# Layer 2 of a four-layer image network: attention of one image issued beside the feed forward of the image ahead, in a fixed order

## The chip, the cores and the metric

The kernel runs on one core of a Trainium2 chip. The core has a matrix engine (TensorE, PE in the profile), a vector engine (VectorE, DVE), an activation engine (ScalarE, ACT), a general engine (GpSimd, POOL) and a queue for transfers (SyncE, SP). Each engine works through its own instructions in order and waits on semaphores for the others. The metric is the device time of one execution in microseconds (us); lower is better. All data are float32, and a product of two float32 matrices is issued as two passes of the matrix engine, so that the profile shows two MATMUL records for each matrix product that is written in the code.

## The reference, cut to what matters

Four layers run one after the other on an input of 4 images with 128 channels of 64 x 64 points: an attention layer, a layer of adder convolutions, the layer that is changed here (layer 2), and a state space layer. Layer 2 is this, for each image on its own:

```python
def _biasfree_ln(x, w):                       # over the 128 channels of a point
    mu = jnp.mean(x, axis=1, keepdims=True)
    var = jnp.mean((x - mu) ** 2, axis=1, keepdims=True)
    return x / jnp.sqrt(var + EPS) * w[None, :, None, None]

def _elgca_attn(x, dw_w, dw_b, qkvl_w, qkvl_b):
    x1, x2 = (x[:, :C2], x[:, C2:])           # C2 = 64 channels each
    x1 = _gelu(_conv(x1, dw_w, dw_b, groups=C2, pad=1))      # 3x3 depthwise
    x2 = _gelu(_conv(x2, qkvl_w, qkvl_b))                    # 64 -> 128 channels
    x2 = x2.reshape(B, HEADS, C4, H, W)                      # q, k, v, lfeat: 32 each
    ...
    qf = _avg_pool_3s2p1(q).reshape(B, C4, -1)
    kf = _max_pool_2s2(k).reshape(B, C4, -1)
    qk = jnp.einsum('bcn,bdn->bcd', qf, kf)                  # 32 x 32
    attn = jnp.swapaxes(jax.nn.softmax(qk, axis=1), 1, 2)
    out = jnp.einsum('bcd,bdn->bcn', attn, v).reshape(B, C4, H, W)
    return jnp.concatenate([x1, lfeat, out], axis=1)

def _elgca_mlp(x, fc1_w, fc1_b, pos_w, pos_b, fc2_w, fc2_b):
    h = _gelu(_conv(x, fc1_w, fc1_b))                        # 128 -> 512 channels
    h = h + _gelu(_conv(h, pos_w, pos_b, groups=h.shape[1], pad=1))
    return _conv(h, fc2_w, fc2_b)                            # 512 -> 128

h = _elgca_attn(_biasfree_ln(x, ln1_w), dw_w, dw_b, qkvl_w, qkvl_b)
out = h + x
return out + _elgca_mlp(_biasfree_ln(out, ln2_w), fc1_w, fc1_b, pos_w, pos_b, fc2_w, fc2_b)
```

## The kernel before, in words

Channels lie on the 128 partitions of the on-chip memory, and the 4096 points of an image along each partition. The four images stay there in tiles `x0` to `x3` (the argument `xp`, 16 KB on each partition) from the residual of layer 1 (`residual`, L578) to the preparation of layer 3 (`layer3_prepare`, L808). Layer 2 (L597 to L775) works in place on them. It loops over the images (L643), and for each image it writes down, in this order:

- The **first layer norm** (`layernorm`, L628) in 8 blocks of 512 points: a matrix product with a matrix of 1/128 gives the mean (`pm`, L633), DVE subtracts (L635), ACT squares (L636), a second product gives the variance (`pv`, L638), ACT takes Ln and Exp (`rstd`, L82 and L83), and DVE multiplies (L641) into the padded tile `hp`.
- The **attention**: 8 matrix products over the upper 64 channels and a Gelu on ACT give `x2` (L654, L657). DVE makes the depthwise convolution of the lower 64 channels in 9 taps over 64 partitions and 4096 points (L664, L666), then ACT makes its Gelu (L667). DVE pools q and k (L672 to L679); PE transposes the pooled maps (L684) and multiplies them (L690); a softmax over a 32 x 32 matrix follows (L694 to L703). DVE adds two parts of the result to the image (L705, L706), and PE and DVE make and add the third in 8 blocks (`po`, L709, and L713).
- The **second layer norm**, into the tile `m` (L716).
- The **feed forward**, in two halves of 32 rows and four chunks of 128 of the 512 channels: `up` is 5 matrix products with a Gelu each into the padded tile `ht` (L734, L737). The depthwise convolution of chunk 0 is made on PE, as 4 x 9 matrix products with diagonal matrices (L747) and a Gelu each (L754). That of chunks 1 to 3 is made on DVE in 9 taps of 128 partitions and 2048 points (L760, L762), with one Gelu on ACT (L765). DVE adds the centre (L766), and 4 matrix products sum the chunk into four banks of the matrix engine's memory (`pf2`, L770). At the end of a half DVE adds the four banks to the image (L775).

The order of instructions on each engine in layer 2 is set by a planner when the kernel is built: it goes by the order in the code as a priority and by estimated costs, and it may take instructions of the next image earlier. Layers 1 and 3 use `tc.keep_in_program_order`, here named `then`, which keeps the instructions given to it in the order of the code on each engine; instructions outside it can be placed freely. Buffers come from pools: `ps` has four banks for all products but the sums, `ps_f` four for the sums; the tiles `hp`, `x2`, `x1`, `cs`, `pf` and `m` exist once, and `ht` and `g` twice.

The activation engine holds one set of function tables at a time. `ln_and_exp` (L76) loads the set with Ln and Exp; a Gelu after it needs another load.

Of the kernel before, what the change touches and what calls it, by code (L numbers as in the profile page):

```python
# [1 line left out]

# [15 lines left out]
B = 4  # L18
# [36 lines left out]
def col(ap):  # L55

    return ap.rearrange("(p o) -> p o", o=1)
# [538 lines left out]

def layer2(tc, cm, xp, ln1, ln2, dw_w, dw_b, qkvl_w, qkvl_b, fc1_w, fc1_b, pos_w, pos_b, fc2_w, fc2_b):  # L597
    nc = tc.nc
    NCH = 4
    with ExitStack() as ctx:  # L600
# [3 lines left out]
        ps = ctx.enter_context(tc.tile_pool(name="l2p", bufs=4, space=PSUM))  # L604
# [8 lines left out]
        ln2_sb = load([1], col(ln2), "ln2")  # L613
        dww = load([TAPS], dw_w, "dww")
        dwb = load([1], col(dw_b), "dwb")
        qw = load([P], qkvl_w, "qw", P // 2)
# [11 lines left out]
        def layernorm(b, w, out, tag):  # L628
            cm.ln_and_exp(tc)
            for k in range(NB):  # L630
                src = inner(xp, b, k)
                pm = ps.tile([P, BK], F32, tag="mm", name=f"pm{tag}{b}_{k}")
                nc.tensor.matmul(pm, cm.mean, src, start=True, stop=True)  # L633
                xc = sb.tile([P, BK], F32, tag="xc", name=f"xc{tag}{b}_{k}")
                nc.vector.tensor_tensor(rows(xc), src, rows(pm), ALU.subtract)  # L635
                nc.scalar.activation(xc, xc, AF.Square)  # L636
                pv = ps.tile([P, BK], F32, tag="mm", name=f"pv{tag}{b}_{k}")
                nc.tensor.matmul(pv, cm.mean, xc, start=True, stop=True)  # L638
                rs = sb.tile([P, BK], F32, tag="rs", name=f"rs{tag}{b}_{k}")
                cm.rstd(nc, rs, pv)  # L640
                nc.vector.scalar_tensor_tensor(out(k), src, w, rows(rs), ALU.mult, ALU.mult)  # L641

        for b in range(B):  # L643
            x_all = xp[b]
            hp = big.tile([P, HP, HP], F32, tag="hp", name=f"hp{b}")
            nc.gpsimd.memset(hp[:, 0:HP:HP - 1, :], 0.0)
            nc.gpsimd.memset(hp[:, 1 : HP - 1, 0:HP:HP - 1], 0.0)
            layernorm(b, ln1_sb, lambda k: hp[:, 1 + RB * k : 1 + RB * (k + 1), 1 : 1 + W], "a")
# [3 lines left out]
            for k in range(NB):  # L652
                pq = ps.tile([P, BK], F32, tag="mm", name=f"pq{b}_{k}")
                nc.tensor.matmul(  # L654
                    pq, qw[64:, :], hp[64:, 1 + RB * k : 1 + RB * (k + 1), 1 : 1 + W], start=True, stop=True
                )
                nc.scalar.activation(x2[:, RB * k : RB * (k + 1), :], rows(pq), AF.Gelu, bias=qb)  # L657

            x1 = big.tile([64, H, W], F32, tag="x1", name=f"x1_{b}")
            for t in range(TAPS):  # L660
                y, x = divmod(t, 3)
                v = hp[0:64, y : y + H, x : x + W]
                if t == 0:
                    nc.vector.tensor_scalar(x1, v, dww[0:64, 0:1], None, ALU.mult)  # L664
                else:
                    nc.vector.scalar_tensor_tensor(x1, v, dww[0:64, t : t + 1], x1, ALU.mult, ALU.add)  # L666
            nc.scalar.activation(x1, x1, AF.Gelu, bias=dwb[0:64])  # L667


            cs = big.tile([64, H, W // 2], F32, tag="cs", name=f"cs{b}")  # L670
            q, kk = slice(0, 32), slice(32, 64)
            nc.vector.tensor_tensor(cs[q], x2[q, :, 0:W:2], x2[q, :, 1:W:2], ALU.add)  # L672
            nc.vector.tensor_tensor(cs[q, :, 1:], cs[q, :, 1:], x2[q, :, 1 : W - 1 : 2], ALU.add)
            nc.vector.tensor_tensor(cs[kk], x2[kk, :, 0:W:2], x2[kk, :, 1:W:2], ALU.max)
            pf = big.tile([64, H // 2, W // 2], F32, tag="pf", name=f"pf{b}")
            nc.vector.tensor_tensor(pf[q], cs[q, 0:H:2, :], cs[q, 1:H:2, :], ALU.add)
            nc.vector.tensor_tensor(pf[q, 1:, :], pf[q, 1:, :], cs[q, 1 : H - 1 : 2, :], ALU.add)
            nc.vector.tensor_scalar(pf[q], pf[q], 1.0 / 9.0, None, ALU.mult)
            nc.vector.tensor_tensor(pf[kk], cs[kk, 0:H:2, :], cs[kk, 1:H:2, :], ALU.max)  # L679

            pff = pf.rearrange("p a c -> p (a c)")
            pt = ps.tile([P, 8, 64], F32, tag="mm", name=f"pt{b}")
            for j in range(8):
                nc.tensor.transpose(pt[:, j, :], pff[:, bass.ts(j, P)], cm.ident[0:64, 0:64])  # L684
            qkt = sb.tile([P, 8, 64], F32, tag="qkt", name=f"qkt{b}")
            nc.vector.tensor_copy(qkt, pt)
            pqk = ps.tile([P, 32], F32, tag="mm", name=f"pqk{b}")
            d = slice(96, 128)
            for j in range(8):
                nc.tensor.matmul(  # L690
                    pqk[d, :], qkt[:, j, 32:64], qkt[:, j, 0:32], start=(j == 0), stop=(j == 7)
                )
            mx = sb.tile([P, 2], F32, tag="mx", name=f"mx{b}")
            nc.vector.tensor_reduce(mx[d, 0:1], pqk[d, :], AX.X, ALU.max, negate=True)  # L694
            ex = sb.tile([P, 32], F32, tag="ex", name=f"ex{b}")
            cm.ln_and_exp(tc)
            nc.scalar.activation(ex[d, :], pqk[d, :], AF.Exp, bias=mx[d, 0:1])
# [745 lines left out]
```

## Time and profile before

| what | us |
|---|---|
| median of 3 runs | 21833.55 (21814.43 to 21852.22) |
| the profiled execution | 21811.67 |
| its span, first to last instruction | 21809.7 |
| layer 2 in it: from the end of the residual to the last write of layer 2 | 17105.7 to 18446.0 |

The profile names groups of instructions by line, engine and operation, and by the tiles they write and read without their numbers (`x<-hp,dww,x` reads `hp`, `dww` and `x`; `x` stands for the image, for `x1` and for `x2`). The page gives the busy time of each engine over the span: PE 19720.1 us (90%), DVE 19100.0 (88%), ACT 17694.9 (81%), POOL 7447.8 (34%). These are averages over layers that differ: layers 0 and 1 end at about 17062 us, layer 2 takes the stretch named above, and layer 3 the rest. In the page's 40 slices of 545 us each, layer 2 lies in slices 32 to 34, where DVE and PE are less busy than before and the DMA engines are idle. A time in a row of the timeline is counted from the start of the span.

### The profile page before, as it was taken

The page shows a single profiled execution, that of the slowest core. Times are in us where ns is not written, and L with a number is a line of the kernel's source. Part 1 is how long each engine was busy: PE and PEld are TensorE (multiplying, and loading weights), DVE is VectorE, ACT ScalarE, POOL GpSimd, SP SyncE. Part 2 cuts the span into 40 slices and gives each one's busy share as a digit, 9 for nine tenths or more (in the row PEclk, how much of TensorE's full clock was granted, in tenths as well). Part 3 has the DMA queues.
Part 4 walks back from the last instruction along what each step waited for, and adds up shares of the span by engine and source line. Part 5 has one row for each costly group of instructions (what it writes and reads, how often), then busy time and mean ns, then how long its engine had stood idle before and what let it go on. Part 6 is the DMA issues. An engine that isn't in the chain of part 4 may idle for free.

```text
span 21809.7 us, 323448 instructions
## 1 busy us (share of the span) xinstructions
PE 19720.1 (90%) x139180; PEld 6260.6 (29%) x139180; DVE 19100.0 (88%) x12244; ACT 17694.9 (81%) x9117; POOL 7447.8 (34%) x3822
## 2 busy tenths in 40 slices
PE   9998999999999999999999999999999656779998
PEld 4443222222222222222222222222222222223333
DVE  7776999999999999979999999999999766589998
ACT  5665999999999999979999999999999422556776
POOL 5664222222222222222222222222222000179998
PEclk9999999999999999999999999999999777689999
DMA  0001777777777777767777777777777200279998
GB/s 12 13 5 37 148 149 144 150 149 145 150 148 147 149 145 150 148 131 144 150 146 146 149 148 144 149 148 147 150 149 148 72 0 9 108 223 249 255 255 219
DMA packets 573938, 2959.29 MB, mean 136 GB/s; under 512 B 163981, under 2 KB 164885, under 8 KB 240213
## 3 DMA queue, kind: packets, MB, share of 16 engines
q0 software_dynamic: 294912, 2147.61, 49.2%
q1 hardware_dynamic: 277012, 782.60, 12.6%
q8 instruction: 1089, 17.84, 0.3%
q10 hardware_dynamic: 576, 8.39, 0.1%
q14 instruction: 349, 2.85, 0.0%
HBM read 662.02 MB, written 128.78 MB: 36 GB/s over the span
## 4 chain that ended last, share of the span: by engine, by line
PE 37%; DMA 29%; DVE 22%; issue 7%; POOL 2%; ACT 2%; SPq 0%; DVEq 0%; POOLq 0%; ACTq 0%
DMA ma<-ma 26%; PE a2pa L424 11%; PE a1pa L424 11%; DVE ma L478 7%; DVE da L469 6%; PE pe L163 4%; PE pav L206 4%; DVE h L1092 3%; DVE g L762 1%; DMA du<-du_d 1%; PE mg L1107 1%; PE pd L747 1%; DMA dl<-delta_d 1%; POOL dbu L1071 1%; DVE aa L461 1%
## 5 line engine op out<-in xcount | busy, mean ns | idle before, releaser
L480 POOL DMA_DIRECT2D ma<-ma x2048 | 3693.6, 1804 | 11187.1 <-DVE ma L478 7337.7
L455 ACT ACTIVATE aa<-a1pb,a1wn 128x4096 f32<-128x4096 f32 x1920 | 6987.3, 3713 | 567.2 <-PE a1pa L424 431.0
L455 ACT ACTIVATE aa<-a2pb,a2wn 128x4096 f32<-128x4096 f32 x1920 | 6979.3, 3711 | 349.9 <-PE a2pa L424 333.0
L424 PE MATMUL a2pa<-aa,a2pick 128*32 128x512 f32 x30720 | 3569.3, 593 | 29.9 <-ACT aa L455 24.8
L424 PE MATMUL a1pa<-aa,a1pick 128*32 128x512 f32 x30720 | 3572.8, 594 | 11.4 <-ACT aa L455 6.2
L469 DVE TENSOR_SCALAR da<-a1pb,a1wa 128x4096 f32<-128x4096 f32 x1408 | 3275.0, 2348 | 293.1 <-PE a1pa L424 292.6
L469 DVE TENSOR_SCALAR da<-a2pb,a2wa 128x4096 f32<-128x4096 f32 x1408 | 3275.3, 2349 | 274.0 <-PE a2pa L424 273.3
L478 DVE TENSOR_SCALAR ma<-a1pb,a1wa 128x2048 f32<-128x2048 f32 x2048 | 2545.0, 1280 | 267.8 <-DMA ma<-ma 266.4
L478 DVE TENSOR_SCALAR ma<-a2pb,a2wa 128x2048 f32<-128x2048 f32 x2048 | 2545.6, 1280 | 262.3 <-DMA ma<-ma 261.1
L424 PE MATMUL a1pa<-da,a1pick 128*32 128x512 f32 x22528 | 2677.9, 597 | 88.2 <-DVE da L469 86.8
L424 PE MATMUL a2pa<-da,a2pick 128*32 128x512 f32 x22528 | 2671.5, 596 | 81.0 <-DVE da L469 79.9
L1107 PE MATMUL mg<-h,ident 128*128 128x512 f32 x4096 | 1953.3, 614 | 197.4 <-ACT m L1116 160.9
L1092 DVE TENSOR_TENSOR_SCAN h<-da,h,dbu 128x1024 f32<-128x1024 f32 x768 | 1804.4, 2349 | 119.0 <-ACT da L1078 25.0
L424 PEld LDWEIGHTS a2pa<-aa,a2pick 128*32 128x32 f32 x30720 | 988.8, 110 | 2362.0 <-issue 2167.7
L424 PEld LDWEIGHTS a1pa<-aa,a1pick 128*32 128x32 f32 x30720 | 992.0, 110 | 2341.8 <-issue 2196.1
L424 PE MATMUL a1pa<-ma,a1pick 128*32 128x512 f32 x8192 | 1090.7, 605 | 334.0 <-DMA ma<-ma 331.7
L424 PE MATMUL a2pa<-ma,a2pick 128*32 128x512 f32 x8192 | 1089.0, 604 | 307.7 <-DMA ma<-ma 305.5
L200 POOL TENSOR_TENSOR ssum<-ssum,et 128x512 f32<-128x512 f32 x960 | 1228.9, 1280 | 233.4 <-ACT et L195 166.5
L424 PEld LDWEIGHTS a1pa<-da,a1pick 128*32 128x32 f32 x22528 | 721.7, 111 | 1835.5 <-issue 1566.0
L424 PEld LDWEIGHTS a2pa<-da,a2pick 128*32 128x32 f32 x22528 | 723.2, 110 | 1820.4 <-issue 1568.7
L1071 POOL TENSOR_TENSOR dbu<-du,B 128x2048 f32<-128x2048 f32 x256 | 1157.0, 4533 | 97.1 <-DMA du<-du_d 45.5
L1120 POOL TENSOR_TENSOR m<-m,C 128x2048 f32<-128x2048 f32 x256 | 1156.8, 4530 | 94.2 <-ACT m L1116 77.5
(294 smaller groups left out, 17845.4 us busy)
## 6 DMA issues: line engine op xcount, KB each, us to landing
ma<-ma POOLq DMA_DIRECT2D x2048, 1024.0 KB, 9.3
dl<-delta_d SPq DMA_DIRECT2D x256, 512.0 KB
dl<-delta_d SPq DMA_DIRECT2D x512, 256.0 KB
du<-du_d SPq DMA_DIRECT2D x256, 512.0 KB
du<-du_d SPq DMA_DIRECT2D x512, 256.0 KB
xs_d<-xs SPq DMA_DIRECT2D x8, 2048.0 KB
sz_d<-sz SPq DMA_DIRECT2D x64, 256.0 KB
delta_d<-dv SPq DMA_DIRECT2D x32, 512.0 KB
```

What stands on the lines that cost most here:

```text
L163: nc.tensor.matmul(pe, k[:, bass.ts(j, P)], unit[u, "q"], start=True, stop=True)
L200: nc.gpsimd.tensor_tensor(unit[u, "sum"], unit[u, "sum"], at, ALU.add)
L206: nc.tensor.matmul(unit[u, "av"], image[u // NB][2][:, j, :], at, start=(j == 0), stop=(j == NJ - 1))
L424: then(nc.tensor.matmul(pa[k][32 * g : 32 * g + 32, :], pick[v][:, 31 - jj : 63 - jj], d[:, bass.ts(4 * at + g, BK)], start=(n // 32, k) n ...
L455: then(nc.scalar.activation(rows(at), view(n, t), AF.Abs, bias=bias, scale=scale))
L469: then(nc.vector.tensor_scalar(rows(dt), view(n, t), weight(n, t), None, ALU.max))
L478: then(nc.vector.tensor_scalar(rows(mt), v, weight(n, t), None, ALU.max))
L480: then(nc.gpsimd.dma_start(ms[1], ms[0], accum_op=ALU.add))
L1071: then(nc.gpsimd.tensor_tensor(t, du, by_states(tiles[n][0], 0, h), ALU.mult))
L1092: then(nc.vector.tensor_tensor_scan(t[:, cols][:, s], da[:, s], st[n, "dbu", h][:, cols][:, s], 0.0 if e % 4 == 0 else st["last"], ALU.mul ...
L1107: then(nc.tensor.matmul(pm, cm.ident, st[n, way, h][:, bass.ts(k, BK)], start=(way == 0), stop=(way == 1)))
L1120: then(nc.gpsimd.tensor_tensor(m, m, by_states(tiles[n][0], 1, h), ALU.mult))
```

## The change

Only layer 2 is changed. Its steps become Python generators (a generator runs to its next `yield` when it is asked for its next step), which two small helpers interleave; nearly every instruction is now given to `then`, so that the order on each engine is that of the code.

The functions `first_norm`, `second_norm`, `attention` and `feed_forward` hold the steps of one image. After the first norm and the attention of image 0, each round b does this: the second norm of image b and the first norm of image b+1, with the last depthwise convolution of image b-1 beside it at one tap for two steps of a norm; then the rest of the feed forward of image b-1 and that of image b up to its last convolution, with one step of the attention of image b+1 beside every second step. The norm itself is in three stages one block apart. In the feed forward the order of chunks is 1, 0, 2, 3; beside each convolution on DVE run the matrix products of a later `up` and those of chunk 0.

Three things change besides the order. The depthwise convolution of the attention is made with the two halves of the image's rows on 128 partitions (`hx`, filled by two transfers of 64 partitions from `hp`), 2048 points each. The two whole-image additions of DVE are made by accumulating transfers of GpSimd's queue, two for each. And buffers change: `ps` has three banks and a new pool `ps_a` one, for the attention; `ht` and `g` exist three times; `x1` shares the place of `cs`.

```diff
+def together(main, beside, ratio):
+    due = 0.0
+    for _ in main:
+        due += ratio
+        while due >= 1.0:
+            due -= 1.0
+            next(beside, None)
...
-        ps = ctx.enter_context(tc.tile_pool(name="l2p", bufs=4, space=PSUM))
+        ps = ctx.enter_context(tc.tile_pool(name="l2p", bufs=3, space=PSUM))
+        ps_a = ctx.enter_context(tc.tile_pool(name="l2a", bufs=1, space=PSUM))
...
+            xcs, rss = {}, {}
+            for s in range(NB + 2):
+                if s < NB:
...
+                    then(nc.tensor.matmul(pm, cm.mean, src, start=True, stop=True))
...
+                    then(nc.vector.tensor_tensor(rows(xc), src, rows(pm), ALU.subtract))
+                    then(nc.scalar.activation(xc, xc, AF.Square))
...
+                k = s - 1
+                if 0 <= k < NB:
...
+                    then(nc.tensor.matmul(pv, cm.mean, xcs.pop(k), start=True, stop=True))
...
+                    then(nc.scalar.activation(rs, pv, AF.Ln, bias=cm.eps))
+                    then(nc.scalar.activation(rs, rs, AF.Exp, scale=-0.5))
...
+                k = s - 2
+                if 0 <= k < NB:
+                    then(nc.vector.scalar_tensor_tensor(
+                        out(k), inner(xp, b, k), w, rows(rss.pop(k)), ALU.mult, ALU.mult
+                    ))
+                yield
...
+        def attention(b):
...
+            hx = big.tile([P, H2 + 2, HP], F32, tag="hx", name=f"hx{b}")
+            for h in range(2):
+                nc.sync.dma_start(hx[64 * h : 64 * h + 64], hp[0:64, H2 * h : H2 * h + H2 + 2, :])
...
+            for h in range(2):
+                half = slice(H2 * h, H2 * h + H2)
+                then(nc.gpsimd.dma_start(x_all[64:96, half, :], x2[64:96, half, :], accum_op=ALU.add))
...
+            def depthwise(t):
                 y, x = divmod(t, 3)
-                v = hp[0:64, y : y + H, x : x + W]
+                v = hx[:, y : y + H2, x : x + W]
...
-            nc.vector.tensor_tensor(x_all[0:64], x_all[0:64], x1, ALU.add)
-            nc.vector.tensor_tensor(x_all[64:96], x_all[64:96], x2[64:96], ALU.add)
             for k in range(NB):
...
+                if k < TAPS - 5:
+                    depthwise(5 + k)
                 o = inner(xp, b, k)[d]
+                then(nc.vector.tensor_tensor(o, o, rows(po[d, :]), ALU.add))
+                if k == TAPS - 6:
+                    then(nc.scalar.activation(x1, x1, AF.Gelu, bias=dwb))
+                    for h in range(2):
+                        then(nc.gpsimd.dma_start(
+                            x_all[0:64, H2 * h : H2 * h + H2, :], x1[64 * h : 64 * h + 64], accum_op=ALU.add
+                        ))
+                yield
...
+            def convolution(half, c, side, per_tap, after):
+                due = 0.0
+                for tap in range(TAPS):
+                    tap_of(half, c, tap)
+                    if tap in after:
+                        after[tap]()
+                    due += per_tap
+                    while due >= 1.0:
+                        due -= 1.0
+                        next(side, None)
+                    yield
+                for _ in side:
+                    pass
+
+            yield from up(0, 1)
             for half in range(2):
...
+                after = {0: lambda: gelu(0, 3), 2: lambda: down(0, 3)} if half else {}
+                yield from convolution(half, 1, chain(up(half, 0), up(half, 2)), 1.2, after)
+                if half:
                     for s in range(4):
+                        result(0, s)
+                        yield
+                dense = on_tensor(half)
+                after = {0: lambda: gelu(half, 1), 2: lambda: down(half, 1)}
+                if not half:
+                    yield from convolution(0, 2, chain(islice(dense, 6), up(0, 3)), 1.25, after)
+                    after = {0: lambda: gelu(0, 2), 2: lambda: down(0, 2), 5: lambda: down(0, 0)}
+                    yield from convolution(0, 3, chain(dense, up(1, 1)), 1.25, after)
+                else:
+                    yield from convolution(1, 2, chain(islice(dense, 6), up(1, 3), dense), 1.9, after)
+            gelu(1, 2)
+            yield "last"
+            yield from convolution(1, 3, iter(()), 0, {})
+            yield "rest"
+            down(1, 2)
+            gelu(1, 3)
+            yield
+            down(1, 0)
+            yield
+            down(1, 3)
+            yield
+            for s in range(4):
+                result(1, s)
+                yield
...
+        for b in range(B):
+            cm.ln_and_exp(tc)
...
+            tail = until(ended, "rest")
+            together(norms(), tail, 0.5)
+            for _ in tail:
+                pass
+            rest, ended = ended, feed_forward(b)
+            beside = attention(b + 1) if b < B - 1 else iter(())
+            together(chain(rest, until(ended, "last")), beside, 0.5)
+            for _ in beside:
+                pass
```

In it, `norms()` is the second norm of image b followed by the first of image b+1; `until(g, mark)` runs a generator up to its mark. `up(half, c)` is five steps, each one product and its Gelu; `on_tensor(half)` is twelve steps of three products each, with a Gelu after every third; `tap_of` is one tap on DVE; `down(half, c)` is the addition of the centre on DVE and four products; `result` is the addition of one bank to the image. The attention of an image is 28 steps: 8 for `x2`, 5 of pooling, 7 with the first five depthwise taps and the softmax among them, and 8 for `po` with the last four taps in the first four.

## The prediction

> **What bounds the kernel now.** The page's averages say nothing of layer 2, so I cut it into the stages of image 0 first, with the table of windows: first norm, attention, second norm, feed forward, and last the whole layer.
>
> ```profile
> core 0: us, PE busy (x) PEld busy (x) DVE busy (x) ACT busy (x) POOL busy (x), PEclk, DMA share, GB/s
> 17105.70:17134.20 28.50, 16.98 (x30) 5.81 (x31) 11.35 (x23) 16.73 (x25) 0.00 (x0) 0.86 0.08 20
> 17134.20:17212.00 77.80, 26.55 (x54) 8.30 (x52) 63.82 (x32) 12.48 (x13) 0.48 (x2) 0.50 0.00 0
> 17212.00:17247.00 35.00, 23.47 (x40) 8.06 (x40) 11.58 (x17) 16.49 (x25) 0.00 (x0) 0.82 0.00 0
> 17247.00:17457.00 210.00, 138.11 (x300) 60.37 (x298) 146.46 (x78) 58.84 (x75) 1.97 (x16) 0.81 0.00 0
> 17105.70:18446.00 1340.30, 763.57 (x1626) 311.20 (x1626) 911.38 (x544) 374.23 (x488) 8.82 (x66) 0.77 0.00 1
> ```
>
> The layer takes 1340.3 us. DVE has the most work, 911, and is idle for 429: in the norms, which are a chain PE, DVE, ACT, PE, ACT, DVE with little overlap, and in the feed forward. The waits of DVE inside the layer say where:
>
> ```profile
> DVE g L766 <- ACT g L754: 200.3, 8, 33.8
> DVE xcb L635 <- PE pmb L633: 74.7, 32, 4.5
> DVE x L713 <- PE po L709: 36.6, 32, 2.1
> DVE xca L635 <- PE pma L633: 31.7, 14, 2.7
> ```
>
> Half of it is one wait, twice an image: chunk 0 goes first, its convolution is on PE, and DVE has nothing else to do (up to 33.8 us). So the layer is bound by DVE's work plus waits that other images' work could fill. I take durations from the groups by shape, from DVE's and PE's order of time, and from the chain of work:
>
> ```profile
> L762 DVE SCALAR_TENSOR_TENSOR g<-ht,pww,g 128x2048 f32<-128x2048 f32 x192 | 444.9, 2348 | 2.9
> L666 DVE SCALAR_TENSOR_TENSOR x<-hp,dww,x 64x4096 f32<-64x4096 f32 x32 | 143.1, 4470 | 0.4
> L705 DVE TENSOR_TENSOR x<-x,x 64x4096 f32<-64x4096 f32 x4 | 17.7, 4417 | 0.1
> L706 DVE TENSOR_TENSOR x<-x,x 32x4096 f32<-32x4096 f32 x4 | 17.7, 4417 | 0.1
> ```
> ```profile
> 17285.40 7.12 DVE L762 SCALAR_TENSOR_TENSOR g<-ht,pww,g 128x2048 f32<-128x2048 f32 x3
> ...
> 17293.64 22.71 DVE L762 SCALAR_TENSOR_TENSOR g<-ht,pww,g 128x2048 f32<-128x2048 f32 x10
> ```
> ```profile
> 17318.60 6.28 PE L770 MATMUL pf<-g,f2w 128*128 128x512 f32 x8 [25.30 <-DVE g L766]
> ...
> 17353.57 3.60 PE L770 MATMUL pf<-g,f2w 128*128 128x512 f32 x8
> 17357.00 16.47 PE L747 MATMUL pd<-ht,diag 128*128 128x512 f32 x38
> ```
> ```profile
> 17132.05 13.32 PE pq L654 x16
> ```
>
> A tap that follows a tap on the same tile starts (7.12-2.35)/2 = 2.39 us after it; with two chunks in turn (the ten) it is (22.71-2.35)/9 = 2.26. A product of two passes at full clock is 16.47/19 = 0.86 us. The eight passes of L770 take 3.60 in a busy stretch, 6.28 after an idle one.
>
> **DVE's work after the change.** The taps of the attention go from 64 x 4096 to 128 x 2048, the shape of L762: from 2.35+8x4.47 = 38.1 us an image to 1.28+8x2.27 = 19.4, 75 us over four images. L705 and L706 leave DVE: 35. The rest stays: 911-110 = 801. By stage and image, in starts from one to the next: attention 36; a norm 8x(0.60+0.67) = 10; a convolution of the feed forward 1.32+7x2.39+2.27 = 20.3; a centre addition (L766) 2.2; the four results 2.7.
>
> **Waits after the change.** The order is fixed, so I walk it.
>
> First norm of image 0: PE's order is now mean of block s, then variance of block s-1, so the loop of 3.42 us a block is cut. The nearest row is layer 3's norm, where Ln, Exp and Square follow at 1.7 us a block; with PE cold at first I take 22 us for the stage (10 work, 12 wait). Attention of image 0, alone: `x2` now has one bank, so PE and ACT take turns: 8x(2.07+0.69+0.15) = 23 instead of 13 us. Pooling 10.6. Five taps with the softmax between them 13, four taps with `po` 12, four `po` alone at 2.9 = 12, and some 3 for the transfer of `x1` at the end: 74 (36 work, 38 wait), against 78 now. Second norm of 0 and first of 1 without a tail: 20 steps of 2.1 = 42 (20, 22).
>
> Feed forward beside an attention, up to its last convolution: DVE has 5x20.3-2+5x2.2+2.7+36 = 150. Where does it wait? (a) First `up`: five products and Gelus, some 5 us; in rounds 1 and 2 the feed forward ahead ends here too, whose 12 products of `down` hold PE 10.3 us while DVE has 6.6 of additions, then results, then `up` with `x2` products between: 12. (b) `down` sits in PE's queue behind DVE's tap 2, so PE stops there; in the second convolution PE then has 3.4 (`down`) + 4x2.57 + 3.6 (`up`) = 17 us against DVE's 14 plus attention steps: 2. (c) In the third, `down(0,0)` needs the last of chunk 0: 3.4+10.3+0.7 = 14.4 after PE's stop, DVE gets there after 10.8: 4. (d) In the last-but-one (`per_tap` 1.9) PE has 12x2.57+3.6+3.4+1.7 = 39.6 us and starts 2 early; DVE has 24. PE also stops for `down`, 2.6. The next norm's mean is behind it all in PE's queue and the norm's subtraction is first in DVE's: 17. That is the largest wait the new order makes. In round 0 the attention runs later and more of it lies beside (d): 12. (e) PE restarts after a stop in (c) and (d), 2.7 each by the row above: 5.
>
> **A rule that speaks against this** is that of the Trainium skill, page "TensorE: Matmul & The Clock Gate", Part 1: after an idle window of about 3.4 us the matrix clock falls to half, until about 3.4 us of sustained work. The new order stops PE at every `down`. By the rule a restart costs 1.7 us, by the row 6.28-3.60 = 2.7; I take the row. Six restarts an image, all on the path, would be 10 us by the rule and 16 by the row; I count two, since elsewhere DVE is the later one. But L654's sixteen passes over 64 rows took 13.32 us and stayed at half, clock 0.50 in that stage, which the 3.4 us alone don't explain; such products now lie between those of the feed forward. This is a rival below.
>
> So, us (work + wait): first norm 22 (10+12); attention 0 74 (36+38); norms 42 (20+22); round 0 177 (150+27); norms with a convolution beside, twice 20+20+5 = 45: 90; rounds 1 and 2 twice 159+40 = 199: 398; last norm 33 (30+3); last round, without attention and with PE as the bound in (b) to (d), and its end, where three `down` and four results follow the last tap: 194 (154+40). Sum 1030, of it DVE's work 799, which agrees with 801. Against 1340: **310 us less**.
>
> **Costs that hide.** Per image four accumulating transfers and two into `hx`. The nearest row:
>
> ```profile
> ma<-ma POOLq DMA_DIRECT2D x2048, 1024.0 KB, 9.3
> ```
>
> `x1`'s two halves are 1024 KB together: 9.3 us if they run together. The Trainium skill's "DMA: Bandwidth & Descriptors", Rules for kernel authors, advises against two transfers to disjoint partition halves: they serialize. By that 18.6 at most. In rounds 0 to 2 either lies under four `po` steps and (d), 20 us and more; in attention 0 the four `po` cover 12, so the rule would add some 9 us once. Taken: the row. `hx` waits under `x2` and the pooling, 33 us. The issue on POOL delays the border writes of a later `ht`, which have several us of slack. If the additions of `po`, which write other partitions of the same image, had to wait for `x1`'s transfer: 10 us an image, 40 in all; nothing in the trace shows such a wait, so 0 to 40, taken 0. Table loads: 1.28 us each on ACT, which is busy 374 of 1340; the tail beside the norms has no ACT work, so norms and Gelus no longer alternate.
>
> The profiled execution was 21811.7, 1.9 above its span; less 310 is 21502. It stands 22 below the median, so for the median 21833.5-310 = 21524, say **21525**.
>
> **Rivals.** (1) *Lockstep costs more.* With one bank and a fixed order each attention step is a round trip of PE behind feed-forward products. For: PE has 9.8 us of products between two `po` in (d) and DVE 7.9. Against: elsewhere DVE has the more. If all waits of the three rounds beside an attention double (107 more) and the cold start spreads, the saving is about 150: 21683. (2) *Waits mostly vanish*, the planner's free instructions and PE running ahead cover (a) to (d): 107 of the 232 less, saving 415: 21420. (3) *PE stays at half clock* in the rounds: a round's products are 131 us at full clock, 262 cold; with 138 before the rounds, 123 of norms and 240 at the end that is 138+3x262+123+240 = 1287: saving about 50, at the edge of the noise and counted inside it. Against: the feed forward now, with stops of 25 us, still has a clock of 0.81. (4) *Slower*: the lockstep of (1) at a price that eats everything. Three attentions of 28 steps are 84 steps; at (310+44)/84 = 4.2 us a step it is slower by more than 0.2%. The worst I find is 2 us on four steps. That the work doesn't overlap at all is (1) and (4) at their limit.
>
> **How the numbers follow.** Forecast 0.74 (own range saving 220 to 390, as the waits go up by 40% or down by 35%), (1) 0.14, (2) 0.06, (3) 0.03, (4) 0.03. About 0.2%, 44 us, is what a measurement can tell from no change. Faster 0.94, same 0.03, slower 0.03. The range takes the forecast's and the near ends of (1) and (2), savings of 185 to 400: 21435 to 21650.
>
> **What would show it.** Right: layer 2 in 1030 us, DVE's work about 800, no idle of 33 us for a Gelu of chunk 0; DVE's longest waits on `pm` at the start of the norms (17 us) and on the centre of chunk 0; a tap of the attention 2.35 us. Wrong: `po` additions waiting for a transfer, a granted clock near 0.5 through the rounds, waits of DVE over 60 us a round, or Ln and Exp with a table load each.

## The result, and the profile after

The changed kernel takes 21566.09 us (median of 4 runs, 21556.91 to 21572.26) against 21826.15 for the kernel before in the same session (median of 4). The ratio is 0.9879, 95% interval 0.9862 to 0.9896: faster by about 260 us, where 21525 had been forecast, 308 below the median shown. The profiled execution took 21570.58 us with a span of 21568.8.

First the table of windows of the kernel after: one stage to a row, in order of time, and the whole layer last. The stages are the first norm of image 0; its attention; second norm of 0 and first of 1; round 0; the norms with a convolution beside them; round 1; norms again; round 2; the last norm, with a convolution; and the last round, which has no attention.

```profile
core 0: us, PE busy (x) PEld busy (x) DVE busy (x) ACT busy (x) POOL busy (x), PEclk, DMA share, GB/s
17117.90:17142.80 24.90, 15.71 (x30) 5.90 (x30) 13.10 (x25) 16.42 (x26) 0.00 (x0) 0.77 0.22 47
17142.80:17209.50 66.70, 31.17 (x55) 6.82 (x56) 38.17 (x31) 12.15 (x14) 4.19 (x12) 0.53 0.24 32
17209.50:17246.00 36.50, 33.47 (x70) 12.44 (x68) 22.72 (x33) 29.46 (x49) 0.00 (x0) 0.93 0.08 16
17246.00:17428.10 182.10, 139.90 (x317) 56.74 (x317) 150.36 (x84) 50.88 (x67) 5.25 (x16) 0.88 0.09 12
17428.10:17475.40 47.30, 31.07 (x63) 11.02 (x61) 40.50 (x43) 30.72 (x50) 0.00 (x0) 0.95 0.06 12
17475.40:17694.90 219.50, 157.56 (x347) 63.89 (x348) 160.13 (x93) 50.00 (x67) 5.58 (x22) 0.84 0.08 10
17694.90:17746.70 51.80, 35.26 (x62) 12.72 (x60) 40.38 (x42) 33.65 (x51) 0.00 (x0) 0.87 0.06 12
17746.70:17968.10 221.40, 161.71 (x347) 65.06 (x348) 160.27 (x93) 49.94 (x67) 5.17 (x20) 0.81 0.07 10
17968.10:18005.40 37.30, 16.49 (x30) 5.54 (x28) 30.23 (x25) 18.94 (x27) 0.00 (x0) 0.74 0.00 0
18005.40:18199.80 194.40, 146.47 (x312) 65.05 (x312) 152.98 (x78) 43.54 (x55) 1.97 (x16) 0.84 0.00 0
17117.90:18199.80 1081.90, 768.81 (x1628) 305.19 (x1628) 808.84 (x537) 335.71 (x466) 22.16 (x86) 0.83 0.07 11
```

Layer 2 went from 1340.3 to 1081.9 us, 258 less, as much as the medians' 260. (The two profiled executions differ by 241 only, 21809.7 to 21568.8: the other layers took 17 us longer in the second one, 12 of them before layer 2 begins, where the code is the same. In the 14 profiles of this record layer 2 begins between 17099.6 and 17137.0.) DVE's work fell from 911 to 809 (799 to 801 forecast), its idle time from 429 to 273 (231 forecast). The waits of DVE in that stretch:

```profile
DVE x L778 <- PE po L772: 81.9, 19, 13.8
DVE g L839 <- ACT ht L806: 40.5, 8, 9.1
DVE g L849 <- ACT g L826: 31.7, 4, 10.8
DVE xcb L656 <- PE pmb L654: 30.2, 16, 6.6
DVE x L861 <- PE pf L855: 26.5, 4, 7.4
DVE cs L712 <- ACT x L702: 19.8, 1, 19.8
```

The wait of 200.3 us for the Gelu of chunk 0 (up to 33.8 each) is down to 31.7. What is largest now did not exist before at this size: 19 waits for `po`, the attention's products, behind those of the feed forward in PE's queue. The groups by shape show the two operations that were replaced:

```profile
L733 DVE SCALAR_TENSOR_TENSOR x<-hx,dww,x 128x2048 f32<-128x2048 f32 x32 | 75.1, 2347 | 0.3
```
```profile
x<-x POOLq DMA_DIRECT2D x8, 512.0 KB, 8.5
x<-x POOLq DMA_DIRECT2D x8, 256.0 KB, 4.4
```

A tap has 2.347 us instead of 4.470, and the two whole-image additions are transfers that land 8.5 and 4.4 us after their issue (medians, each of a half); DVE waits for neither.

### The profile page after: what moved, and what is told of

The parts are those of the page before. It is cut to its first block, busy times and chain, and to the rows that moved or that the text cites. A ratio compares the mean times of both kernels' runs of the same rounds, so it can differ in the third digit from the quotient of the medians.

```text
span 21568.8 us, 323508 instructions
## 1 busy us (share of the span) xinstructions
PE 19748.3 (92%) x139180; PEld 6262.4 (29%) x139180; DVE 18995.3 (88%) x12236; ACT 17656.1 (82%) x9094; POOL 7459.1 (35%) x3838
## 4 chain that ended last, share of the span: by engine, by line
PE 37%; DMA 29%; DVE 22%; issue 7%; ACT 2%; POOL 2%; SPq 1%; DVEq 0%; POOLq 0%; ACTq 0%
DMA ma<-ma 26%; PE a2pa L425 11%; PE a1pa L425 11%; DVE ma L479 7%; DVE da L470 6%; PE pe L164 4%; PE pav L207 4%; DVE h L1257 4%; DVE g L841 1%; DMA dl<-delta_d 1%; PE mg L1272 1%; DMA du<-du_d 1%; POOL dbu L1236 1%; DVE aa L462 1%; PE pd L820 1%
## 6 DMA issues: line engine op xcount, KB each, us to landing
dl<-delta_d SPq DMA_DIRECT2D x512, 256.0 KB
du<-du_d SPq DMA_DIRECT2D x512, 256.0 KB
sz_d<-sz SPq DMA_DIRECT2D x64, 256.0 KB
```

## The experiments

Each kernel has one profiled execution. A saving in layer 2 is 1340.3 us less its layer 2; it has no interval of its own, so the saving of the whole program, by the medians against the kernel before of the same session, stands beside it. They agree within 14 us. How well layer 2 repeats can be seen where six of these kernels hold the same instructions: from its start to the second norm of image 0 they take 93.0 to 95.4 us. So differences of 8 and 12 us in layer 2 are read below only together with the waits that moved.

| kernel | layer 2, us | saved there | saved, by medians | ratio to before, 95% interval |
|---|---|---|---|---|
| after | 1081.9 | 258 | 260 | 0.9879, 0.9862 to 0.9896 |
| e1_attention_alone | 1163.7 | 177 | 173 | 0.9923, 0.9908 to 0.9938 |
| e2_old_operations | 1169.4 | 171 | 164 | 0.9925, 0.9910 to 0.9939 |
| e3_dense_earlier | 1052.9 | 287 | 283 | 0.9872, 0.9857 to 0.9887 |
| e4_two_banks | 1070.4 | 270 | 271 | 0.9876, 0.9859 to 0.9892 |
| e5_operations_alone | 1270.5 | 70 | 72 | 0.9969, 0.9957 to 0.9980 |
| e6_attention_sooner | 1106.8 | 234 | 246 | 0.9893, 0.9876 to 0.9909 |
| e7_next_up_first | 1036.1 | 304 | 314 | 0.9857, 0.9842 to 0.9872 |
| e8_together | 1035.9 | 304 | 300 | 0.9862, 0.9847 to 0.9876 |
| e9_norm_as_before | 1171.5 | 169 | 164 | 0.9926, 0.9911 to 0.9941 |
| e10_both | 1025.9 | 314 | 314 | 0.9858, 0.9843 to 0.9873 |
| e11_attention_later | 1062.9 | 277 | 291 | 0.9871, 0.9856 to 0.9885 |
| e12_later_two_banks | 1033.5 | 307 | 302 | 0.9865, 0.9848 to 0.9881 |

### Which part of the change is worth what

**The attention not beside the feed forward, but whole ahead of it:**

```diff
             rest, ended = ended, feed_forward(b)
             beside = attention(b + 1) if b < B - 1 else iter(())
-            together(chain(rest, until(ended, "last")), beside, 0.5)
             for _ in beside:
                 pass
+            for _ in chain(rest, until(ended, "last")):
+                pass
```

> Each attention of images 1 to 3 is issued whole ahead of its round instead of beside it; all else as in the changed kernel, whose layer 2 takes 1082 us in the profile. Theory (the attention beside the feed forward hides only its own waits, 28.5 of the 66.7 us that attention 0 takes alone, and does not fill the waits of the feed forward): attention 67 us three times, feed forward alone 161 + 174 + 174 by the last round's stretch, together 710 against 623 now: layer 2 about 1168, +86 us. Rival (the gain comes from the fixed order and the norms; the place of the attention is worth little): +20 or less. Second rival (the attention also fills the feed forward's waits, about 48 us a round): +150 or more.

Layer 2 is 82 us longer, near the theory's 86. Counted from the start of one second norm to the next, it is 44 us in round 0 (217.6 to 261.3), but 24 and 17 in rounds 1 and 2 (266.4 to 290.1, 273.2 to 289.9). Hiding an attention pays about half as much in the rounds that begin with the end of another feed forward, so I looked for the fault there.

**The order of the change with the old operations** (taps over 64 partitions, additions on DVE):

```diff
-            x1 = big.tile([P, H2, W], F32, tag="cs", name=f"x1_{b}")
+            x1 = big.tile([64, H, W], F32, tag="cs", name=f"x1_{b}")
...
-                v = hx[:, y : y + H2, x : x + W]
+                v = hp[0:64, y : y + H, x : x + W]
...
-                    for h in range(2):
-                        then(nc.gpsimd.dma_start(
-                            x_all[0:64, H2 * h : H2 * h + H2, :], x1[64 * h : 64 * h + 64], accum_op=ALU.add
-                        ))
+                    then(nc.vector.tensor_tensor(x_all[64:96], x_all[64:96], x2[64:96], ALU.add))
+                if k == NB - 1:
+                    then(nc.vector.tensor_tensor(x_all[0:64], x_all[0:64], x1, ALU.add))
```

> The order of the changed kernel with the attention's operations of before: depthwise taps of 64 partitions x 4096 points and the two whole-image additions on DVE (the addition of x1 after the last po). DVE gets 38.1 - 19.6 + 8.8 = 27 us more an image. Theory (outside the last-but-one convolution of a round DVE is the bound): image 0 +25 in the open, rounds 0 to 2 +21 each, as 6 us fall where DVE waits for PE: +88 us. Rival (the rounds are bound by PE and by waits, DVE's work is free there): +25 to +35, image 0 alone.

87 us longer than after, as the theory had it (88): the order alone, with its buffers, saves 171, the operations on top of it 87, out of 107 us of DVE's work (916 to 809).

**The operations alone, in the planner's order:**

```diff
+            hx = big.tile([P, H // 2 + 2, HP], F32, tag="hx", name=f"hx{b}")
+            for h in range(2):
+                nc.sync.dma_start(hx[64 * h : 64 * h + 64], hp[0:64, H // 2 * h : H // 2 * h + H // 2 + 2, :])
...
-                v = hp[0:64, y : y + H, x : x + W]
+                v = hx[:, y : y + H // 2, x : x + W]
...
-            nc.vector.tensor_tensor(x_all[0:64], x_all[0:64], x1, ALU.add)
-            nc.vector.tensor_tensor(x_all[64:96], x_all[64:96], x2[64:96], ALU.add)
+            for h in range(2):
+                half = slice(H // 2 * h, H // 2 * h + H // 2)
+                nc.gpsimd.dma_start(x_all[64:96, half, :], x2[64:96, half, :], accum_op=ALU.add)
+                nc.gpsimd.dma_start(x_all[0:64, half, :], x1[64 * h : 64 * h + 64], accum_op=ALU.add)
```

> The kernel before, its planner and its order left as they are, with the change's operations only: the attention's taps on 128 partitions (from two transfers into hx) and the two whole-image additions by accumulating transfers. DVE's work falls by 110 us in both theories (911 to about 800). The order alone was worth 171 us of the 258 and the operations on top of it 87. Rival (the two parts simply add): layer 2 about 87 us shorter than before, 1253. Theory (some of the freed time turns into waits, since here the attention lies alone and the transfers of hx, some 9 us, and of x1, 8.5 us behind its Gelu, are covered by nothing): about 50 us shorter, between 30 and 90, layer 2 some 1290.

They save 70, between the two sizes expected (50 and 87) and inside the theory's range. DVE's work fell by 108 (911.4 to 803.6); 38 came back as waits, and the waits of DVE in layer 2 name two that the kernel before did not list:

```profile
DVE x L669 <- DMA hx<-hp: 17.9, 4, 4.5
...
DVE mx L703 <- ACT ex L702: 13.7, 4, 3.4
```

DVE waits 4.5 us an image for the transfer into `hx` when the attention has nothing around it, and 3.4 for the softmax; the transfer of `x1`, which I had expected to cost, shows no wait. In the fixed order neither wait for `hx` nor one of that size for the softmax appears. So the prediction's "hides" for `hx` is right, and its price without that cover is 18 us in four images. The two parts do not merely add (171 + 70 = 241): the order also hides what the operations need.

**The norm's loop as it was**, variance of the block before ahead of the mean of this one, in the fixed order:

```diff
             for s in range(NB + 2):
+                k = s - 1
+                if 0 <= k < NB:
+                    pv = ps.tile([P, BK], F32, tag="mm", name=f"pv{tag}{b}_{k}")
+                    then(nc.tensor.matmul(pv, cm.mean, xcs.pop(k), start=True, stop=True))
...
                 if s < NB:
...
-                k = s - 2
+                k = s - 1
                 if 0 <= k < NB:
                     then(nc.vector.scalar_tensor_tensor(
```

> The kernel after with the loop of the norm as it was (the variance of the block before ahead of the mean of this one, two stages), in the fixed order. The norm alone had 3.42 us a block before and 1.75 to 2.2 after, in 24 blocks, 28 to 40 us; 40 blocks lie beside the taps of a convolution, where PE, DVE and ACT follow each other twice a block behind a tap of 2.35 us. Theory: layer 2 is 50 to 85 us longer, taken 65: that part of the 171 us of the order is the norm's loop. Rival: the taps cover the longer chain, at most 25 us longer.

89 us longer, over the top of the theory's range and far from the rival. DVE in order of time, second norm of image 0, first with the old loop, then after:

```profile
17264.79 0.69 DVE L664 TENSOR_TENSOR xcb<-x,pmb 128x512 f32<-128x512 f32 x1 [2.08 <-PE pmb L662]
17265.40 0.74 DVE L669 SCALAR_TENSOR_TENSOR m<-x,ln,rsb 128x512 f32<-128x512 f32 x1
17268.22 0.69 DVE L664 TENSOR_TENSOR xcb<-x,pmb 128x512 f32<-128x512 f32 x1 [2.08 <-PE pmb L662]
```
```profile
17220.75 0.69 DVE L656 TENSOR_TENSOR xcb<-x,pmb 128x512 f32<-128x512 f32 x1
17221.70 0.75 DVE L669 SCALAR_TENSOR_TENSOR m<-x,ln,rsb 128x512 f32<-128x512 f32 x1 [0.27 <-ACT rsb L665]
17222.50 0.69 DVE L656 TENSOR_TENSOR xcb<-x,pmb 128x512 f32<-128x512 f32 x1
```

3.43 us from one block to the next against 1.75. The convolution beside later norms does not cover it: from the first subtraction to the last, the pairs of norms with a convolution take 60 and 66 instead of 41 and 46 us, the pair without one 59 instead of 30. So the old loop sets the pace even with taps between its steps: the 40 blocks beside a convolution lost some 50 us, not the 30 that the expectation left for them.

The attention beside (82), the norm's loop (89) and the operations (87) add up to the whole 258. That leaves nothing for the new order of chunks and the convolution beside the norms, but undoing parts one at a time does not divide a gain: where two parts fill the same wait, each looks smaller. What those two are worth alone was not tried.

### Where the missing 52 us went

**Half of chunk 0's products in the second half moved one convolution earlier:**

```diff
-                yield from convolution(half, 1, chain(up(half, 0), up(half, 2)), 1.2, after)
+                dense = on_tensor(half)
+                if half:
+                    side, per_tap = chain(up(1, 0), up(1, 2), islice(dense, 6)), 1.9
+                else:
+                    side, per_tap = chain(up(0, 0), up(0, 2)), 1.2
+                yield from convolution(half, 1, side, per_tap, after)
...
-                    yield from convolution(1, 2, chain(islice(dense, 6), up(1, 3), dense), 1.9, after)
+                    yield from convolution(1, 2, chain(up(1, 3), dense), 1.25, after)
```

> In the second half the first six steps of chunk 0's convolution on PE run beside the first convolution on DVE instead of the second. Theory (PE has 51 us of products beside the last-but-one convolution of rounds 1 and 2 where DVE has 24, and DVE waits 28 us in all on po and on the norm's mean): 15.4 us of products move to a place where PE is idle; rounds 1 and 2 lose 15 to 20 us each, round 0 about 10, the last round about 0 to 4: -45 us (-30 to -60). Rival (these waits are round trips through the one bank of the attention, whatever PE has to do): -10 to +5.

29 us shorter, just under the theory's range; the rival is out. From norm to norm, rounds 1 and 2 are 15 and 17 us shorter, as expected, but round 0 only 1, where 10 were expected. The waits for `po` fall from 81.9 to 56.7 and those for the norm's mean from 30.2 to 14.9. The crowding of PE in the last-but-one convolution, place (d), is a cause.

**Two banks for the attention and two for the rest:**

```diff
-        ps = ctx.enter_context(tc.tile_pool(name="l2p", bufs=3, space=PSUM))
-        ps_a = ctx.enter_context(tc.tile_pool(name="l2a", bufs=1, space=PSUM))
+        ps = ctx.enter_context(tc.tile_pool(name="l2p", bufs=2, space=PSUM))
+        ps_a = ctx.enter_context(tc.tile_pool(name="l2a", bufs=2, space=PSUM))
```

> Two banks for the attention's products and two instead of three for the others. Theory (PE's amount of work in the last-but-one convolution is the cause): po can be issued one step earlier, but the work is the same: rounds -5 to +10 each for want of the third bank; attention 0 gains some 8 us in x2 and in the last four po: -10 to +20 in all. Rival (the round trip through one bank is the cause): the waits on po, 82 us in the trace, fall by half or more: -40 us.

12 us shorter, 9 of them at `x2` of image 0 (19.8 to 10.8 us), where nothing else runs. The waits for `po` fall from 81.9 to 68.1 only, where the rival wanted half, and those for the norm's mean rise from 30.2 to 41.7. The one bank, rival (1)'s reason, costs little in the rounds, at least when its second is taken from the other products.

**The attention sooner, and later:**

```diff
-            together(chain(rest, until(ended, "last")), beside, 0.5)
+            together(chain(rest, until(ended, "last")), beside, 0.6)
```

> The kernel after with the attention at 60 steps to 100 of the feed forward, so that it ends before the third convolution of the second half. Theory (there PE is the later engine, and DVE's work beside it is free): the wait moves from po to the start of the norms, with more than 20 us in rounds 1 and 2, and the four additions that now lie where DVE is the later engine cost their own time: layer 2 0 to 20 us longer. Rival (the round trips of po are what costs there): layer 2 15 to 45 us shorter.

```diff
-            together(chain(rest, until(ended, "last")), beside, 0.5)
+            together(chain(rest, until(ended, "last")), beside, 0.46)
```

> The kernel after with the attention 46 steps to 100 of the feed forward instead of 50, so that its last po additions and taps end some five steps later, inside the second half's third convolution, where PE is the later engine by some 20 us. Theory: DVE's work there is free, so layer 2 is 10 to 25 us shorter, and the wait of DVE for po in rounds 1 and 2 falls. Rival: the later po are still round trips of PE in the same stretch, and layer 2 is within 6 us of 1082 or longer.

Sooner is 25 us longer, later 19 us shorter. The wait for the norm's mean, of the sooner, the later in this order:

```profile
DVE xcb L656 <- PE pmb L654: 76.3, 16, 18.9
```
```profile
DVE xcb L656 <- PE pmb L654: 13.3, 16, 2.1
```

With the attention sooner DVE waits less for `po` (44.4) and more for the norm's mean (76.3), by more than is won. The two runs fit this account: PE has a fixed load in (d), what DVE does in its shadow costs nothing, and an attention that ends too soon leaves the shadow empty. Later also helps just where it should: the rounds 1 and 2, norm to norm, go from 266.4 and 273.2 to 255.4 and 256.0, while round 0, whose attention had ended after the last tap already, gets 8 us longer, with a new wait of 8.4 for `x2`. But the account does not cover all of it. Of the 25 us of the sooner run, 13 are in round 0, and only 9 are the sum of the two waits; those for the first tap's `ht` and for chunk 0's Gelu grow by 15 (40.5 to 50.5 and 31.7 to 36.5). A pace moves every step of the attention, not only the last ones.

**The next image's first `up` ahead of the last products of the feed forward before it** (its results go beside the first convolution):

```diff
+            next(rest, None)
             yield from up(0, 1)
+            next(rest, None)
...
+                    after = {t: lambda: next(rest, None) for t in (3, 4, 5, 6)}
...
-            together(chain(rest, until(ended, "last")), beside, 0.5)
+            together(until(ended, "last"), beside, 0.55)
```

> The kernel after, with the first up of the next image issued ahead of the last products of the feed forward before it, whose results move beside the first convolution: DVE's centre additions come first, and the Gelus of the up run while PE makes the sums. In the kernel after DVE waits 6.5 us for pf and 9.1 us for ht at each of these places. Theory: these 16 us fall to about 5, so layer 2 is about 11 us shorter in rounds 1 and 2 each and a few in the last round: about 25 us in all. Rival: PE is the bound there (the same products are made in either order) and the wait moves to the first tap of the convolution or to the results: 0 to 8 us in all.

46 us shorter, nearly twice the theory. The waits tell why: at place (a), `pf`, `ht` and an unnamed one at the same tap, they fall by 21 us (26.5 + 40.5 to 6.1 + 17.9 + 22.1), near the 25 expected. The other 23 are at `po` and the norm's mean (112.1 to 89.1). The edit took the seven steps of the rest out of the count by which the attention is paced, so in rounds 1 and 2 the attention ends two taps of the feed forward later. That was not meant; by the two runs before it may explain the 23, but no run has this edit with the pace kept.

**Both edits, with a sooner attention and with the pace back** (in both, the diagonal matrices are made after the first norm; the diffs show what differs between the two):

```diff
+            for _ in until(ended, "up"):
+                pass
+            together(until(ended, "last"), beside, 0.75)
```

> The kernel after with three edits: half of the dense products of chunk 0 in the second half one convolution earlier (29 us on its own), the next up ahead of the last products (25 expected on its own), the attention begun at the first convolution with three steps to four of the feed forward, and the diagonal matrices made after the first norm, which waits 8.0 us for their transfer. If the waits are separate, the gains add: layer 2 about 60 to 80 us shorter than in the kernel after, 1000 to 1020. If PE has become the bound in the rounds, the gain stays near that of the moved products alone, 30 to 40 us.

```diff
+            together(until(ended, "last"), beside, 0.55)
```

> The kernel after with the two edits that each shortened layer 2 alone, the moved products of chunk 0 (29 us) and the next up first (46 us), the attention's pace close to that of the kernel after (11 steps to 20) and the diagonal matrices after the first norm (which moves no work). The same two edits with an attention of three steps to four gained 46 only (layer 2 1036). Theory: there the attention had ended before the convolution in which PE is the later engine, and DVE waited for the norm's mean instead (48.8 us); with the pace back, the gains add to 60 to 80 us: layer 2 1000 to 1022. Rival: after either edit PE is the bound in the rounds, and the place of the attention makes no odds: 1030 to 1042.

The first is 46 us shorter than after, no more than one of its two edits alone and between its two expectations. With the pace back it is 56: neither the theory's 60 to 80 nor the rival's 40 to 52. The waits show what was counted twice. (a) falls by 22, and `po` with the norm's mean by 33.5 (112.1 to 48.0 + 30.6): nearly the 56, as the smaller changes cancel. The first edit alone had taken 31 from `po` and the start of the norms, the second 23 from the same waits; both together take hardly more than the first. Moving the diagonal matrices won a little: the 8.0 us before them are gone, and the longest wait at the first norm's subtractions rose from 4.0 to 8.3; from the start of layer 2 to the second norm of image 0 both kernels take 89 us instead of 93 to 95.

**The same with two banks and a pace of 0.52:**

> The kernel with the moved products and the next up first together (layer 2 1025.9) with two more edits: two banks for the attention and two for the rest instead of one and three, which was worth 12 us on its own, and 52 steps of the attention to 100 of the feed forward instead of 55, so that its last additions lie some three steps later, where PE is the later engine. If the gains add: 9 us at x2 of image 0 and some 5 from the pace, layer 2 about 1010 (1000 to 1020), with DVE's wait for x2 of image 0 near 11 us. If the other products miss their third bank beside the doubled dense products, or the later additions run on past the convolutions: 1026 or more.

The second case of the expectation: 8 us longer than the run above in layer 2, though the wait for `x2` of image 0 fell from 19.4 to 9.3 as expected. The 18 us it lost are in the rounds (`po` 48.0 to 68.2), half of them in round 0. Whether the third bank or the pace does it was not separated. The version with both edits and one bank, 21511.04 us (21497.69 to 21516.73), has the lowest median of the kernels run, about 54 us below after (314 saved against 260); that with the next `up` first (21515.13, also 314 saved) can't be told from it.

## Why the prediction was right, and where it was off

The sign, the place and the mechanism were right, and the time lies inside the range, 41 us above the forecast. One sign that it had named for being wrong was met: DVE waits 61 us in round 2, just over the 60 (59 in round 1). By its own stages, the sum was 1030 and came out at 1082:

- **DVE's work**: 809 against 799 (the terms of the sum add to 798). The eight taps with a sum save 68 (143.1 to 75.1), the first one 4 and the additions 35, 107 of the 110 forecast; most of the rest is the feed forward's taps, 192 as before with the same mean but 451.0 us busy instead of 444.9: before, taps on two chunks in turn overlapped a little (2.26 us from start to start, 2.35 long).
- **Before the rounds**: first norm 24.9 (22 forecast; DVE waits 8.0 for the transfer of the weights behind the diagonal matrices, a wait that the kernel before does not list), attention of image 0 66.7 (74; `x2` took about the 23 forecast, and at the end nothing waits for the transfer of `x1`, for which it had 3), norms 36.5 (42). Together 128 against 138: these 10 us hide part of the miss below, by luck.
- **Round 0 and the last round**: 182 (177) and 194 (194).
- **Norms with a convolution**: 47.3 and 51.8 (45 each), the last 37.3 (33). Together 13 too low.
- **Rounds 1 and 2**: 219.5 and 221.4 (199 each). These 43 us are most of the 52.

Inside round 1 the work is right (160.1 against 159), the waits are not, 59 against 40: (a) 15.7 against 12; (b) 0 against 2; (c) 7.3 against 4 and a restart of 2.7; a wait of 5.6 at the first `po`, which was not in the walk; and (d) 27.8 against 17. The step that failed is (d), in its size. PE's order of time there, round 1:

```profile
17642.37 10.88 PE L820 MATMUL pd<-ht,diag 128*128 128x512 f32 x18
...
17659.60 6.51 PE L855 MATMUL pf<-g,f2w 128*128 128x512 f32 x8 [5.37 <-DVE g L849]
17665.95 7.89 PE L820 MATMUL pd<-ht,diag 128*128 128x512 f32 x18
...
17678.39 15.62 PE L820 MATMUL pd<-ht,diag 128*128 128x512 f32 x36
```

The first eighteen products took 10.88, a later eighteen 7.89: PE came to them slow, after stopping between the `po` before. Then it stopped 5.37 at `down`, forecast at 2.6, because DVE had itself waited 7.4 for `po`; and it restarted slow again, 6.51 for eight instead of 3.60. So PE needed 51 us from 17642.4 to 17693.8, where 39.6 + 2.6 less a start 2 early gave 40: two restarts of 3, a stop longer by 2.8, and no early start. I had allowed two restarts an image, but only one of them here. DVE's side, where these 11 us become waits:

```profile
17654.27 0.69 DVE L778 TENSOR_TENSOR x<-x,po 32x512 f32<-32x512 f32 x1 [7.38 <-PE po L772]
...
17675.60 0.69 DVE L778 TENSOR_TENSOR x<-x,po 32x512 f32<-32x512 f32 x1 [13.79 <-PE po L772]
...
17694.90 0.69 DVE L656 TENSOR_TENSOR xcb<-x,pmb 128x512 f32<-128x512 f32 x1 [6.61 <-PE pmb L654]
```

The forecast had looked for one wait of 17 at the norm; 21 of the 27.8 come at two `po`. With (a) and (d) both treated, the rounds 1 and 2 of the run with both edits take 246 us from norm to norm, where the forecast's sum is 199 + 45 = 244. That a reordered kernel meets this number shows that the two places are large enough for the miss; it does not show each term.

**The clock.** The 1.7 us for a restart, an estimate from the rule of the Trainium skill ("TensorE: Matmul & The Clock Gate", Part 1), was set aside for the row's 2.7; the restarts in (d) cost 3.0 and 2.9 (10.88 - 7.89 and 6.51 - 3.60), so the row was the better guide, and still a little low. That the slowdown becomes general, rival (3), is out: the granted clock is 0.81 to 0.88 in the rounds.

**The other rivals.** (1), all waits of the rounds doubled, is out: they came to 59 and 61 instead of 40 in rounds 1 and 2, and to 32 instead of 27 in round 0. The excess lies where it had looked, at `po` in (d), but the run with two banks gives little support to its reason, the one bank. (2), waits vanish, and (4), slower, are out. Rival (4)'s price of 4.2 us for each of 84 steps is far off: with no attention at all beside the feed forward the layer is only 82 us longer, so interleaving gains about 1 us a step. **What hides**: no wait for an accumulating transfer appears in layer 2, so the 0 taken for `po` behind `x1`'s transfer was right. The two halves of `x1`, issued together, land 7.4 to 9.9 us after their issue, as the row of 9.3 has it; the 18.6 that the prediction gave as the most does not appear. **Table loads**: norms and Gelus alternate no more, 18 loads of 1.28 us in layer 2 where the groups of before show 41.

## What to carry to other kernels

When work is interleaved in a fixed order, find first which engine is the later one in each stretch, and put the other engine's free work there: ending the attention five taps later in rounds 1 and 2 was worth 19 us, five taps sooner (seven in round 0) cost 25, while the second bank was worth 12. A wait that moves when you move work (`po` to the norm's mean) is one wait; count it once when adding up the gains of two edits. And a loop of several engines is cheapest with one more stage: putting the next block's mean ahead of this one's variance gave 1.75 instead of 3.43 us a block where nothing ran beside it, and undoing it cost 89 us, a third of this change.

## What the runs showed of the hardware that was not expected

The products of `x2` over 64 rows, with stops of only 0.8 us between them, lose PE's clock in the attention of image 0. PE in order of time, kernel after:

```profile
17144.08 1.12 PE L699 MATMUL pq<-hp,qw 64*128 64x512 f32 x2 [2.38 <-ACT x L702]
17145.98 1.63 PE L699 MATMUL pq<-hp,qw 64*128 64x512 f32 x2 [0.78 <-ACT x L702]
17148.38 2.07 PE L699 MATMUL pq<-hp,qw 64*128 64x512 f32 x2 [0.78 <-ACT x L702]
```

1.12 us becomes 2.07 within 5 us and stays; the stage has a granted clock of 0.53. None of the stops reaches the 3.4 us of the rule that the prediction weighed. Neither the 64 rows nor the stops decide it alone. In the kernel before, the same products run without a stop, and PE's rows for images 0 and 1 are these:

```profile
17131.98 13.38 PE L654 MATMUL pq<-hp,qw 64*128 64x512 f32 x16
...
17470.08 7.22 PE L654 MATMUL pq<-hp,qw 64*128 64x512 f32 x16
```

Image 0 (the 13.32 us that the prediction read) is slow from its third pass on, with records of 1.06 us where image 1 has 0.59, and twelve more us of unbroken products do not bring the clock back: 0.53 is granted in this stretch. Images 1 to 3 take 7.22 us each, image 1 at a granted clock of 1.00. In the kernel after, the eight pairs of round 1, among products of the feed forward, take 1.12 us each. So what PE did before must count as well; which part of it does is open.

And a place to read with care: in the kernel with the next `up` first, DVE's idle time of 8.5 us before the first tap is put down to "issue", nothing that the profile shows, though the last Gelu that writes the tap's `ht` ends at 17497.57 and the tap begins at 17497.66; the order of time names what the label doesn't.
